# Moving a few element-wise operations of a fused kernel's set-up from VectorE to GpSimd

## The chip, the cores and the metric

The kernel runs on one core of one Trainium2 chip. A core has five engines that each work through their own list of instructions in order and wait for one another by semaphores: TensorE (PE in the profile, with its weight loads as PEld), VectorE (DVE), ScalarE (ACT), GpSimd (POOL) and SyncE (SP, which here only issues transfers). The metric is the device time of one execution in microseconds, as a median of runs.

## The reference, cut to what matters

The program is one gated cross-attention block followed by a mixture of experts, for 8 sequences (x: 8 x 512 x 256, context: 8 x 1024 x 192). The part that the change touches prepares a convolution filter (an S4D kernel) from parameters alone, once for all sequences:

```python
dt = jnp.exp(log_dt)
A = A_re + 1j * A_im                                # 256 x 64
dtA = dt[:, None] * A
dC = C * (jnp.exp(dtA) - 1.0) / A
powers = jnp.exp(dtA[:, :, None] * jnp.arange(L))   # L = 512
K = 2.0 * jnp.einsum('dn,dnl->dl', dC, powers).real
y = irfft(rfft(x) * rfft(K))[:, :L] + x * D_skip
```

Beside it, and independent of it, stands attention in which each row of scores (1024 wide, 4 heads) keeps its 32 largest entries, takes a softmax over them and is averaged over the heads. Later stages need both: attention's result modulates the normalised x, the filter is applied in the frequency domain, and then come a feed-forward layer, one shared expert and one of 8 routed experts per token.

## The kernel before, in words

**The loop over sequences.** At line 1394 the kernel runs several streams side by side for each sequence b: the attention of b (`attention`, line 905), the layers behind the attention of b - 1 (`behind`), and the preparation of b + 1 (`prepare`, line 431). For b = 0 there is nothing behind it, and its place is taken by `setup` (line 604), which computes the filter and loads the small weights. So the set-up lies beside the attention of the first sequence, and must be over before `mixed` (line 1057) of sequence 0 can use the filter (`kf`, line 556).

**The set-up.** Its first part works on 128 x 256 tiles, all of them slices of one tile `us` (`small`, line 676) or of `ats` (the four transposed parameters) and `dds`. It ends in the coefficient dC, whose real and imaginary parts `dcr` and `dci` become `uu` and `vv`, two slices of `dds`. Then comes a loop of 8 steps over 32 channels each (line 731). The power exp(dtA l) is split into l = 32 a + c. Each step builds, for 16 values of a, the angles' tiles `ta`, `tk` and the growth `tp` (128 x 512), and for 32 values of c the tiles `qa`, `qk`, `qq` (128 x 1024). GpSimd makes the products with the indices, VectorE reduces the angle to one turn (a rounding into `tk` or `qk`, and a subtraction), ScalarE takes sines and exponentials, and then `tk` and `ta` are scaled by `uu` and `vv`, added (line 750) and multiplied into `tp`; on the other side `qq` is multiplied by `qk` (line 762). TensorE multiplies `qq` with `tp` into `pz`, 32 small products a step, and ScalarE copies the result into `ktime`. After the last step come two rounds of matrix products with the Fourier table, which give `kf`.

**Attention.** A step works on 128 rows and two of the four heads, so a sequence takes 8 steps. TensorE makes the scores `pS`, ScalarE copies them to `sc`, VectorE pairs them by maximum and minimum into `mn`, reduces into `hi`, and GpSimd prunes with two integer operations on `mn` (lines 944 and 945). VectorE then finds the largest eight of a row four times (MAX8 and MATCH_REPLACE8), ScalarE takes exponentials into `e`, VectorE masks and sums them (`e<-sc,t,e`), ScalarE scales them, and GpSimd adds the heads into `acc` (line 983). At the end of 128 rows TensorE transposes `acc` (`pa`) and multiplies it with the context `cx` into `pu`.

**The order of the work.** Nothing is issued while the kernel's functions run. Each operation is noted with an estimated cost (`time`, line 137), and `order` (line 220) then lists them as a planner does: it goes through time, and gives each engine, among the operations that could begin, the one with the smallest number in the order of the streams. The costs enter only there. Each engine then works through its own list strictly in order. So changing an operation's engine changes the two lists directly and, by the planner's times, the order of others. Tiles come from pools with few buffers: `ta`, `tk`, `tp` have two each, `qa` and `qk` one each, and `qq` takes its turn with the weights of later layers in a pool of five.

**Line numbers.** Almost all operations go through one helper, so the profile gives them all line 323. They are told apart by their tiles.

Of the kernel before, what the change touches and what calls it, by code (L numbers as in the profile page):

```python
# [334 lines left out]
def bc(ap, axis, n):  # L335

    ap = ap.unsqueeze(axis)
    shape = list(ap.shape)
    shape[axis] = n
    return ap.broadcast_to(shape)  # L340
# [3 lines left out]
def tile_kernel(ctx: ExitStack, tc: tile.TileContext, a: dict, out: bass.AP):  # L344
# [45 lines left out]
    V, S, GP, TE, SY = (plan.engine(n, e) for n, e in (  # L390
        ("DVE", nc.vector), ("ACT", nc.scalar), ("POOL", nc.gpsimd), ("PE", nc.tensor), ("SP", nc.sync)))
# [4 lines left out]
    def bank(name, pool=ps_mm, tag="mm"):  # L396
        return pool.tile([P, 512], F32, tag=tag, name=name)
# [206 lines left out]
    def setup():  # L604
# [58 lines left out]
        ar, ai, cr, ci = (at[n] for n in ("A_re", "A_im", "C_re", "C_im"))  # L663
# [12 lines left out]
        def small(tag):  # L676
            return us[:, int(tag[1]), :]
# [13 lines left out]
        er, ei = small("u2"), small("u0")  # L691
# [4 lines left out]
        xr, xi, w1 = small("u3"), small("u4"), small("u1")  # L696
        V.tensor_mul(xr, cr, er)
        V.tensor_mul(w1, ci, ei)
        V.tensor_sub(xr, xr, w1)
        V.tensor_mul(xi, cr, ei)  # L700
        V.tensor_mul(w1, ci, er)
        V.tensor_add(xi, xi, w1)
        a2, w2 = small("u5"), small("u2")
        V.tensor_mul(a2, ar, ar)
        V.tensor_mul(w2, ai, ai)
# [2 lines left out]
        dcr, dci = small("u0"), small("u1")  # L708
# [1 line left out]
        V.tensor_mul(w2, xi, ai)  # L710
        V.tensor_add(dcr, dcr, w2)
        V.tensor_mul(dcr, dcr, a2)
        V.tensor_mul(dci, xi, ar)
        V.tensor_mul(w2, xr, ai)
        V.tensor_sub(dci, dci, w2)
        V.tensor_mul(dci, dci, a2)


        lo, hi = slice(0, NST), slice(NST, 2 * NST)
# [11 lines left out]
        for s in range(D // DC):  # L731
            ds = slice(s * DC, (s + 1) * DC)

            def big(pool, tag, n, name):
                return pool.tile([P, DC * n], F32, tag=tag, name=f"{name}{s}").rearrange(
                    "p (d n) -> p d n", n=n)


            ta, tk, tp = big(pk, "ga", NA, "ta"), big(pk, "sg", NA, "tk"), big(pk, "t2", NA, "tp")
            GP.tensor_mul(ta, bc(tn[:, ds], 2, NA), bc(ioa, 1, DC))  # L740
            GP.tensor_mul(tp, bc(dr[:, ds], 2, NA), bc(ioa, 1, DC))
            V.tensor_scalar(tk, ta, MAGIC, MAGIC, ALU.add, ALU.subtract)
            V.tensor_sub(ta, ta, tk)
            S.activation(tk, ta, AF.Abs)
            S.activation(tk, tk, AF.Sin, bias=hpi, scale=-2.0 * PI_IN)
            S.activation(ta, ta, AF.Sin, scale=2.0 * PI_IN)
            S.activation(tp, tp, AF.Exp)
            GP.tensor_mul(tk, tk, bc(uu[:, ds], 2, NA))
            GP.tensor_mul(ta, ta, bc(vv[:, ds], 2, NA))
            V.tensor_add(tk, tk, ta)  # L750
            GP.tensor_mul(tp, tp, tk)

            qa, qk, qq = big(pr, "xe", NCC, "qa"), big(pr, "hT", NCC, "qk"), big(wpool, "w", NCC, "qq")
            GP.tensor_mul(qa, bc(tn[:, ds], 2, NCC), bc(ioc[:, :NCC], 1, DC))
            GP.tensor_mul(qq, bc(dr[:, ds], 2, NCC), bc(ioc[:, :NCC], 1, DC))
            V.tensor_scalar(qk, qa, MAGIC, MAGIC, ALU.add, ALU.subtract)
            V.tensor_sub(qa, qa, qk)
            S.activation(qk[lo], qa[lo], AF.Abs)
            S.activation(qk[lo], qk[lo], AF.Sin, bias=hpi[lo], scale=-2.0 * PI_IN)
            S.activation(qk[hi], qa[hi], AF.Sin, scale=2.0 * PI_IN)  # L760
            S.activation(qq, qq, AF.Exp)
            V.tensor_mul(qq, qq, qk)
            pz = bank(f"pz{s}")
            for d in range(DC):
                TE.matmul(pz[:NCC, d * NA : (d + 1) * NA], qq[:, d, :], tp[:, d, :],
                          start=True, stop=True)

            z = pz[:NCC].rearrange("p (d t j) -> p j t d", t=NF, j=NA // NF)
            for j in range(NA // NF):
                S.copy(ktime[j * NCC : (j + 1) * NCC, :, ds], z[:, j])  # L770
            yield
# [621 lines left out]
    for b in range(B):  # L1393
        streams = [(some(att, n_att), n_att), behind(b - 1) if b else (setup(), n_set)]
        if b + 1 < B:
            streams.append((states[b + 1].prep, n_prep))
        together(*streams)
# [84 lines left out]
```

## Time and profile before

The time before is 1792.7 us, the median of 3 runs (1792.55 to 1793.37). The profiled execution took 1794.11 us, of which the page's span (first to last instruction) is 1792.3 us.

| | busy us | share of the span |
|---|---|---|
| PE | 1513.1 | 84% |
| DVE | 1302.1 | 73% |
| ACT | 1154.6 | 64% |
| POOL | 931.5 | 52% |

The averages hide the stages. The set-up loop runs in the window from about 65 to 227 us; a table by window stands in the prediction. In the answers below, a line of a group or of a timeline reads: engine, operation, output tile, inputs, sizes, number of instructions, busy time and mean; in brackets or after the bar, the idle time of the engine just before it and what ended that. A tile's answer gives the shortest, median and longest of its instructions, and when the first and the last began.

### The profile page before, as it was taken

What the parts mean: (1) busy time and instruction counts of PE and PEld (TensorE: products, weight loads), DVE (VectorE), ACT (ScalarE), POOL (GpSimd) and SP (SyncE); (2) the same over time, 40 slices, a digit from 0 to 9 for tenths busy, and PEclk for the clock granted to TensorE, in tenths of its full rate; (3) what the DMA queues carried; (4) which work ended last, traced back from release to release, by engine and by line L of the source; (5) the groups of instructions that cost most, each with busy time, mean ns of one, the idle gap of its engine ahead of it and who ended that gap; (6) DMA issues with size and microseconds to landing.
All of it is one profiled execution on the core that took longest, in us unless ns stands there. A gap on an engine that the chain in (4) does not pass through costs nothing. (4 is left out here: it accounts for less than half of the span.)

```text
span 1792.3 us, 21191 instructions
## 1 busy us (share of the span) xinstructions
PE 1513.1 (84%) x6363; PEld 893.1 (50%) x6363; DVE 1302.1 (73%) x3073; ACT 1154.6 (64%) x2008; POOL 931.5 (52%) x1072
## 2 busy tenths in 40 slices
PE   5365577797998798999889999998999989889885
PEld 2143333344543454465436554654465547547685
DVE  6989977885878697977798889697978987222210
ACT  4778844676747774887578877885788678123121
POOL 5578544445363645465555765474557646233122
PEclk8555677786998799998989999998999989989898
DMA  4000110001200120143103330431033205523794
GB/s 118 0 1 24 33 35 18 12 12 47 70 20 12 47 65 18 36 128 96 54 12 109 91 102 12 135 107 58 12 111 107 66 12 162 179 103 86 228 280 117
DMA packets 101289, 131.68 MB, mean 73 GB/s; under 512 B 9687, under 2 KB 73004, under 8 KB 101166
## 3 DMA queue, kind: packets, MB, share of 16 engines
q1 hardware_dynamic: 93102, 121.05, 21.1%
q0 software_dynamic: 7008, 8.42, 2.6%
q8 instruction: 52, 0.85, 0.2%
q10 hardware_dynamic: 1056, 0.79, 0.1%
q14 instruction: 71, 0.58, 0.1%
HBM read 112.22 MB, written 18.78 MB: 73 GB/s over the span
## 5 line engine op out<-in xcount | busy, mean ns | idle before, releaser
L323 PE MATMUL pS<-kT,qT 32*128 32x512 f32 x512 | 285.6, 742 | 71.2 <-DVE mn L323 61.0
L323 POOL TENSOR_TENSOR acc<-acc,e 128x1024 f32<-128x1024 f32 x96 | 229.0, 2385 | 182.3 <-ACT e L323 179.9
L323 DVE MAX8 top<-mn 128x8 f32<-128x256 f32 (+1 forms) x512 | 276.0, 556 | 11.9
L323 ACT COPY sc<-pS 128x512 f32<-128x512 f32 x256 | 145.6, 584 | 167.1 <-PE pS L323 136.9
L323 DVE SCALAR_TENSOR_TENSOR e<-sc,t,e 128x1024 f32<-128x1024 f32 x128 | 180.3, 1421 | 40.6 <-ACT e L323 40.3
L323 DVE TENSOR_TENSOR mn<-sc,pS 128x512 f32<-128x512 f32 x256 | 165.2, 677 | 35.9 <-PE pS L323 19.9
L323 POOL TENSOR_TENSOR mn<-mn 128x256 int32<-128x256 int32 x128 | 102.4, 800 | 164.4 <-DVE hi L323 163.8
L323 PEld LDWEIGHTS pS<-kT,qT 32*128 32x128 f32 x512 | 75.9, 208 | 203.6 <-DVE mn L323 98.9
L323 ACT ACTIVATE e<-sc,sm 128x1024 f32<-128x1024 f32 x128 | 145.1, 1146 | 16.1 <-POOL acc L323 13.2
L323 ACT ACT_TABLE_LOAD x118 | 151.4, 1283 | 4.0 <-issue 2.0
L323 PE MATMUL pm<-hT,w 128*128 128x512 f32 x256 | 137.9, 677 | 13.6 <-ACT hT L323 13.6
L323 ACT ACTIVATE junk<-sc,sm 128x1024 bf16<-128x1024 f32 x128 | 146.1, 1141 | 1.3
L323 PEld LDWEIGHTS pu<-aT,cx 128*96 128x96 f32 x1024 | 122.2, 168 | 28.6 <-issue 24.1
L323 PE MATMUL pu<-aT,cx 128*96 128x128 f32 x1024 | 135.4, 282 | 0.2 <-ACT aT L323 0.2
L323 PE MATMUL am<-w,ga 128*128 128x256 f32 x512 | 129.1, 398 | 6.1 <-ACT ga L323 6.1
L323 PEld LDWEIGHTS am<-w,ga 128*128 128x128 f32 x512 | 96.9, 196 | 51.4 <-issue 27.6
L323 POOL DMA_INDIRECT out_dram<-yb,to x38 | 61.5, 1620 | 96.7 <-DMA out_dram<-yb,to 46.3
L323 ACT ACTIVATE e<-e,sm 128x1024 f32<-128x1024 f32 x96 | 108.5, 1147 | 1.6 <-DVE sm L323 1.6
L323 POOL TENSOR_TENSOR mn<-mn,hi 128x256 int32<-128x256 int32 x128 | 104.9, 819 | 8.0
L323 DVE TENSOR_TENSOR ger<-sgr,pu 128x512 f32<-128x512 f32 x38 | 26.0, 684 | 108.7 <-PE pu L323 105.9
L323 DVE MATCH_REPLACE8 mn<-top,mn 128x256 f32<-128x256 f32 x256 | 104.6, 409 | 0.0
L323 POOL TENSOR_TENSOR yf<-yf,t 128x512 f32<-128x512 f32 (+1 forms) x80 | 85.2, 1089 | 35.0 <-DVE t L323 33.7
(287 smaller groups left out, 3125.0 us busy)
## 6 DMA issues: line engine op xcount, KB each, us to landing
rt_gate<-in_L_ffn_rt_gate_dram SPq DMA_DIRECT2D x38, 512.0 KB
rt_up<-in_L_ffn_rt_up_dram SPq DMA_DIRECT2D x38, 512.0 KB
rt_down<-in_L_ffn_rt_down_dram SPq DMA_DIRECT2D x38, 512.0 KB
w<-in_L_xattn_W_dram SPq DMA_DIRECT2D x32, 512.0 KB
cx<-in_ctx_dram SPq DMA_DIRECT2D x7, 768.0 KB
xtab<-zt SPq DMA_DIRECT2D x8, 642.5 KB
xb<-xtab SPq DMA_DIRECT2D x38, 128.5 KB
xt<-in_x_dram SPq DMA_DIRECT2D x8, 512.0 KB
```

The source lines that it names most:

```text
L323: o.fn()
```

## The change

In the loop, the addition of the two angle terms into `tk` (128 x 512) and the product of `qq` with `qk` (128 x 1024) go from VectorE to GpSimd, in each of the 8 steps. In the first part, seven operations on 128 x 256 go the same way: three that make `xi`, and four that make `dci`. As two engines would now write the same scratch slice, a new slice `w3` (the eighth of `us`, unused so far) is taken for the moved ones. Results, tiles and transfers are otherwise the same.

```diff
-        V.tensor_mul(xi, cr, ei)
-        V.tensor_mul(w1, ci, er)
-        V.tensor_add(xi, xi, w1)
+        w3 = small("u7")
+        GP.tensor_mul(xi, cr, ei)
+        GP.tensor_mul(w3, ci, er)
+        GP.tensor_add(xi, xi, w3)
...
-        V.tensor_mul(dci, xi, ar)
-        V.tensor_mul(w2, xr, ai)
-        V.tensor_sub(dci, dci, w2)
-        V.tensor_mul(dci, dci, a2)
+        GP.tensor_mul(dci, xi, ar)
+        GP.tensor_mul(w3, xr, ai)
+        GP.tensor_sub(dci, dci, w3)
+        GP.tensor_mul(dci, dci, a2)
...
             GP.tensor_mul(ta, ta, bc(vv[:, ds], 2, NA))
-            V.tensor_add(tk, tk, ta)
+            GP.tensor_add(tk, tk, ta)
             GP.tensor_mul(tp, tp, tk)
...
             S.activation(qq, qq, AF.Exp)
-            V.tensor_mul(qq, qq, qk)
+            GP.tensor_mul(qq, qq, qk)
```

## The prediction

> **What bounds the kernel now.** I read the page first (DVE and PE high, shares that are averages over stages), then a table of windows, since the change touches only the set-up. The four windows run from the second attention step of sequence 0 (its first `mn` at 69.8 us) to the first `mn` of sequence 1 (273.5 us):
>
> ```profile
> 69.80:121.30 51.50, 27.67 (x186) 17.67 (x187) 44.05 (x74) 35.14 (x57) 34.46 (x27) 0.52 0.00 1
> 121.30:172.20 50.90, 25.17 (x219) 15.96 (x218) 47.52 (x79) 44.12 (x70) 39.66 (x25) 0.55 0.07 21
> 172.20:223.00 50.80, 31.79 (x196) 18.96 (x195) 46.70 (x72) 44.19 (x69) 31.13 (x22) 0.58 0.10 29
> 223.00:273.50 50.50, 36.33 (x154) 16.83 (x152) 40.55 (x103) 23.75 (x43) 21.79 (x23) 0.76 0.10 32
> sum 203.70, PE 120.96 PEld 69.42 DVE 178.82 ACT 147.19 POOL 127.04; mean PE 30.24 PEld 17.36 DVE 44.71 ACT 36.80 POOL 31.76
> ```
>
> Columns after the length: busy us of PE, PEld, DVE, ACT and POOL, TensorE's granted clock, the share of DMA, GB/s. VectorE is busy 178.8 of 203.7 us (88%), GpSimd 127.0 (62%), ScalarE 147.2 (72%). TensorE mostly waits, and no transfer matters (DMA share 0.10 or less). So VectorE is the fullest engine of this stage, but ScalarE is not far behind. Later TensorE is:
>
> ```profile
> 700.00:900.00 200.00, 187.25 (x734) 105.92 (x733) 164.81 (x410) 151.01 (x264) 116.02 (x138) 0.95 0.24 70
> 1300.00:1500.00 200.00, 190.24 (x807) 115.31 (x806) 169.33 (x419) 155.76 (x258) 114.51 (x133) 0.97 0.25 76
> ```
>
> From there on nothing changes: set side by side, the planned lists of all engines are alike from the first attention step of sequence 1 to the end, and differ only before it. The later weights' loads start when a tile comes free, so they move with the work. I therefore carry a shift of the 273.5 us point to the end one to one. The chain of waits shown on the page reaches back only to 1646 us, so it says nothing against or for this.
>
> **What is removed from VectorE.** The groups of 50 to 275 us:
>
> ```profile
> L323 DVE SCALAR_TENSOR_TENSOR e<-sc,t,e 128x1024 f32<-128x1024 f32 x16 | 24.9, 1579 | 0.0
> L323 DVE TENSOR_TENSOR qq<-qq,qk 128x1024 f32<-128x1024 f32 x8 | 13.8, 1726 | 5.4 <-ACT qk L323 5.4
> L323 DVE TENSOR_TENSOR qa<-qa,qk 128x1024 f32<-128x1024 f32 x8 | 13.4, 1672 | 0.2
> L323 DVE TENSOR_TENSOR ta<-ta,tk 128x512 f32<-128x512 f32 x8 | 12.9, 1616 | 0.2
> L323 DVE TENSOR_SCALAR qk<-qa 128x1024 f32<-128x1024 f32 x8 | 9.0, 1129 | 0.4 <-POOL qa L323 0.4
> L323 DVE TENSOR_TENSOR tk<-tk,ta 128x512 f32<-128x512 f32 x8 | 9.0, 1126 | 6.2 <-POOL ta L323 6.0
> L323 DVE TENSOR_SCALAR tk<-ta 128x512 f32<-128x512 f32 x8 | 7.5, 935 | 0.0
> ```
>
> The product `qq<-qq,qk` takes 13.8 us and the sum `tk<-tk,ta` 9.0: 22.8 us of work. VectorE also idles 5.4 and 6.2 us just before these two, because it reaches them before their inputs are there: 11.6 us of idle time that leave its list with them. The seven small operations on 128 x 256 take, by the timeline, 1.18 us (0.75 for two, 0.43 for one) for `xi` and 1.63 for `dci`: 2.8 us. GpSimd's `xi` needs about 2.2 us, while VectorE does `xr` and the 1/|A|^2 part (over 3 us), so VectorE hardly waits for it; `dci`, some 2.9 us on GpSimd, runs beside `dcr`, but then `uu` and `vv` need it. I take 2 of the 2.8 us (bounds -1, if the wait for `dci` outlasts the saving, and 2.8).
>
> **What is added to GpSimd.** No row has these two there. The nearest are GpSimd's two-input products of the same sizes, and VectorE's own as a yardstick (shortest, median, longest ns):
>
> ```profile
> L323 POOL TENSOR_TENSOR tk<-tk,dds x8: 1053/1058/2035, 82.1 to 211.3; 128x512 f32<-128x512 f32 x8
> L323 POOL TENSOR_TENSOR qa<-us,ioc x8: 1907/2500/2951, 66.6 to 208.4; 128x1024 f32<-128x1024 f32 x8
> L323 DVE TENSOR_TENSOR qq<-qq,qk x8: 1224/1322/2928, 86.6 to 220.5; 128x1024 f32<-128x1024 f32 x8
> ```
>
> Undisturbed, a step adds 1.06 + 1.91 = 2.97 us, 8 steps 23.8; by the means of these groups in the stage (1.20 and 2.45) 29.2. The Trainium skill speaks against the move: "GPSIMD Engine Reference", section 4.1, Engine selection, gives element-wise work to VectorE, GpSimd being about 2 times slower with two inputs. The shortest times here say 1907/1224 = 1.56. By the rule the undisturbed addition would be an estimated 2 x 8 x (1.22 + 0.67) = 30 us; by the rows 24, with the collisions of this stage 29. I take 27. The seven small ones add 7 x 0.73 = 5.1 us before the stage (a 96 x 256 product takes 0.73). GpSimd becomes 127.0 + 27 = 154 us: 79% of a stage of 194. It issues no transfer in this stage, so none is held up. On the SP queue nothing is added; four small loads (`b`, `vt`) come to stand ahead of four large weight loads, which takes away GpSimd's 17 us wait for `b`, worth nothing, as what follows it was ready only then.
>
> **What the remaining work of VectorE loses.** The two engines get in each other's way:
>
> ```profile
> 159.69 2.72 DVE L323 SCALAR_TENSOR_TENSOR e<-sc,t,e 128x1024 f32<-128x1024 f32 x1
> ```
>
> ```profile
> 158.38 2.95 POOL L323 TENSOR_TENSOR qa<-us,ioc 128x1024 f32<-128x1024 f32 x1 [1.64 <-ACT qk L323]
> ```
>
> Alone they take 1.27 and 1.91 us. MAX8, MATCH_REPLACE8 and operations that read scores from `pS` keep their times beside GpSimd; those with two inputs in SBUF, and the roundings, do not. Their excess over the shortest of their kind: e 24.9 - 16 x 1.27 = 4.6; qa 13.4 - 8 x 1.22 = 3.6; ta 12.9 - 8 x 0.69 = 7.4; qk 9.0 - 8 x 0.68 = 3.6; tk 7.5 - 8 x 0.41 = 4.2: 23.4 us. GpSimd's busy share goes from 62% to 79%, times 1.27: 6 us more. The skill's "SBUF — State Buffer", section "SBUF: two separate sides", calls this an exclusive lock held for a whole instruction. If every added us on GpSimd kept VectorE out, that would be 27, which would eat the move; but VectorE's operations of this kind have only 42 us of undisturbed work in the stage (14 x 1.27 + 8 x 3.0), about a fifth of the time, and a fifth of 27 is 5.4. Both ways about 6; bounds 3 and 15.
>
> **New waits.** This is the term with the widest bounds. Attention's pruning (`mn` on GpSimd, 14 pairs in the stage) stands in the same in-order list, now behind up to one product and one sum more; behind it wait MATCH_REPLACE8 on VectorE, then the exponentials' masks, ScalarE's scaling and the next `pS`. Such a wait exists already:
>
> ```profile
> 235.45 0.09 DVE L323 MATCH_VALUE_LOAD mn<-top,hi 128x8 f32 x1 [3.14 <-POOL mn L323]
> ```
>
> If each of 14 prunings meets half of a step's added 2.97 us, that is 21 us. The other way, too: `qq` is now in GpSimd's list behind waits for sines (`qk` from ScalarE), and holds what is behind it. And the planned list puts the last step of the loop later against attention: the last `pz` now stands behind scores of sequence 1, and VectorE's `kf` work behind the third block's masks, so VectorE can idle for the chain product, `pz` (3.6 us), copy (1.0), first Fourier product (1.9). Against that, ScalarE has four table loads fewer in its list (15 for 19, 4 x 1.28 = 5 us). From 0 (the planner interleaves the waits with other work) to 35 us; I take 20, near the 21.
>
> **Sum.** 22.8 + 11.6 + 2 removed, 6 and 20 added: 10.4 us less. The profiled execution's span would be 1792.3 - 10.4 = 1781.9 us, its time 1794.1 - 10.4 = 1783.7; the median lies 1.4 under that execution, so 1782.3, which I call 1782.5.
>
> **The rivals.**
> - *GpSimd becomes the fullest engine and holds attention up* (slower). Of its 76.7 us idle, 17 are the wait for `b`; the waits for ScalarE, TensorE and VectorE in its list make up the rest, about 59. If they stay, the stage takes 154 + 59 = 213 us instead of 203.7: 9 us slower, some 1802. It decides when new waits pass 30 us, 2.1 us a pruning. For it: the list is in order, and the sum and the product wait for ScalarE. Against: 79% is less than the 88% at which VectorE ran.
> - *The waits eat the gain* (30 us, within 3.6): about 1792.5. The engines' shares would then be even at about 80%, which is hard to pack in order.
> - *The waits are well hidden*, 5 us: 25 us less, about 1767. ScalarE's 142 us in a stage of 179 (79%) would allow it.
> - *The shift does not reach the end*: TensorE is the limit later and had work left over. Against: TensorE's lists need attention of sequence 0 and the filter first, and it idled in the stage. I give it no number of its own; it falls under "the same".
>
> **How the numbers follow.** Likeliest, about 10 us less: 0.50; well hidden: 0.11; the same: 0.14; slower: 0.25. The likeliest alone spans 1777 to 1789, faster than the 3.6 us (0.2%) that a measurement can tell from none. So faster 0.61, same 0.14, slower 0.25. For 8 in 10, the range goes from 1768 (most of the well-hidden case) to 1802 (the slower case's own number); what is left out is half of each.
>
> **What would show it.** Right: the first `mn` of sequence 1 near 263 us; VectorE busy about 162 us in the stage up to there, GpSimd about 154; the sum at 1.1 to 1.3 us and the product at 1.9 to 2.5 on GpSimd; VectorE's waits for GpSimd's `mn` some 20 us; later windows alike. Wrong: waits for `mn` over 30 us; a product well over 2.5 us; VectorE's excess over 30 us; or an early shift that shrinks between 300 and 1500 us.

## The result, and the profile after

The changed kernel takes 1798.35 us in the median, the kernel before, on the same chip, 1793.03: a ratio of 1.0035 with a 95% interval of 1.002 to 1.005. That is 5 to 6 us slower where 10 us faster was forecast. One of its 14 runs, at 2982.85 us, counts as slow and is left out of the ratio. The profiled execution of the changed kernel took 1795.14 us with a span of 1793.4 (before: 1794.11 and 1792.3). Two comparisons of the same two kernels differ by a quarter of a per cent (a second one, below, gave 1.0011), so what I say of the change is that it gains nothing and costs some 2 to 6 us; the interval of the second comparison also holds no change at all.

The stage in which the prediction was made, from the second attention step of sequence 0 to the first `mn` of sequence 1, now runs from 70.56 to 275.61 us. I call the end of it the join. The table by windows of the kernel after, four quarters of the stage (columns as before):

```profile
70.56:121.80 51.24, 30.11 (x181) 18.45 (x182) 41.94 (x78) 35.81 (x56) 39.36 (x29) 0.50 0.00 1
121.80:173.10 51.30, 25.80 (x163) 13.55 (x163) 45.58 (x75) 39.38 (x63) 42.31 (x28) 0.57 0.06 21
173.10:224.30 51.20, 29.70 (x192) 18.11 (x190) 41.80 (x73) 39.45 (x68) 42.17 (x31) 0.60 0.06 19
224.30:275.61 51.31, 36.45 (x219) 19.43 (x219) 38.53 (x85) 26.84 (x46) 31.83 (x26) 0.80 0.13 42
sum 205.05, PE 122.06 PEld 69.54 DVE 167.85 ACT 141.47 POOL 155.66; mean PE 30.52 PEld 17.38 DVE 41.96 ACT 35.37 POOL 38.92
```

VectorE went from 178.82 us of work to 167.85, GpSimd from 127.04 to 155.66: the work did move. But the stage is 1.4 us longer, and VectorE now idles 205.05 - 167.85 = 37.2 us in it, where it idled 24.9. No engine is full any more: 82%, 76% and 69% for VectorE, GpSimd and ScalarE. The later windows are as they were:

```profile
700.00:900.00 200.00, 187.05 (x734) 105.69 (x733) 164.64 (x409) 149.56 (x262) 114.17 (x137) 0.95 0.24 70
1300.00:1500.00 200.00, 190.31 (x791) 113.88 (x790) 169.33 (x416) 154.29 (x257) 114.41 (x130) 0.97 0.25 75
```

The groups of 50 to 275 us of the kernel after, those that answer to the ones shown of before:

```profile
L323 DVE SCALAR_TENSOR_TENSOR e<-sc,t,e 128x1024 f32<-128x1024 f32 x16 | 27.0, 1694 | 9.4 <-ACT e L323 9.3
L323 POOL TENSOR_TENSOR qq<-qq,qk 128x1024 f32<-128x1024 f32 x8 | 20.0, 2498 | 1.3 <-ACT qk L323 1.2
L323 DVE TENSOR_TENSOR qa<-qa,qk 128x1024 f32<-128x1024 f32 x8 | 16.5, 2061 | 0.3
L323 DVE TENSOR_TENSOR ta<-ta,tk 128x512 f32<-128x512 f32 x8 | 15.4, 1926 | 0.2
L323 POOL TENSOR_TENSOR tk<-tk,ta 128x512 f32<-128x512 f32 x8 | 10.8, 1349 | 0.6
L323 DVE TENSOR_SCALAR tk<-ta 128x512 f32<-128x512 f32 x8 | 9.1, 1142 | 0.3 <-POOL ta L323 0.3
L323 DVE TENSOR_SCALAR qk<-qa 128x1024 f32<-128x1024 f32 x8 | 8.5, 1057 | 2.4 <-POOL qa L323 2.4
```

Three things are to be seen. The two moved operations cost GpSimd 20.0 + 10.8 = 30.8 us. The operations that stayed on VectorE grew: `qa` from 13.4 to 16.5, `ta` from 12.9 to 15.4, the rounding `tk` from 7.5 to 9.1, `e` from 24.9 to 27.0. And the mask `e`, which before did not wait (0.0 in its row), now waits 9.3 us for ScalarE. In the view of waits (VectorE, 65 to 280 us) the first rows of the kernel before were

```profile
DVE tk L323 <- POOL ta L323: 6.0, 4, 3.1
DVE qq L323 <- ACT qk L323: 5.4, 5, 2.3
DVE mn L323 <- POOL mn L323: 3.5, 2, 3.1
```

and those of the kernel after put the wait for ScalarE first, ahead of GpSimd's `mn`, which I had expected to lead:

```profile
DVE e L323 <- ACT e L323: 9.3, 5, 3.5
DVE mn L323 <- POOL mn L323: 7.8, 1, 7.8
DVE wf L323 <- PE p_wf L323: 5.7, 3, 3.5
DVE kf L323 <- PE pf L323: 4.4, 1, 4.4
```

(Columns: us in total, times, the longest.) The one wait for `mn` is of the kind foreseen. This is GpSimd's timeline in front of it, with the sum and the product in the way:

```profile
106.42 1.26 POOL L323 TENSOR_TENSOR tk<-tk,ta 128x512 f32<-128x512 f32 x1
107.76 1.27 POOL L323 TENSOR_TENSOR tp<-tp,tk 128x512 f32<-128x512 f32 x1
109.46 2.35 POOL L323 TENSOR_TENSOR qq<-qq,qk 128x1024 f32<-128x1024 f32 x1 [0.42 <-ACT qk L323]
111.77 0.72 POOL L323 TENSOR_TENSOR mn<-mn 128x256 int32<-128x256 int32 x1
```

VectorE stood for the prune until 112.52 (idle 7.76 us). The waits for ScalarE are of another kind. VectorE's timeline:

```profile
204.91 0.74 DVE L323 MAX8 top<-hi 128x8 f32<-128x256 f32 x2
209.12 1.56 DVE L323 SCALAR_TENSOR_TENSOR e<-sc,t,e 128x1024 f32<-128x1024 f32 x1 [3.47 <-ACT e L323]
```

and ScalarE's at the same time:

```profile
197.06 1.28 ACT L323 ACT_TABLE_LOAD   x1
198.35 0.72 ACT L323 ACTIVATE tk<-tk,hpi 128x512 f32<-128x512 f32 x1
...
202.35 0.61 ACT L323 ACTIVATE ta<-ta 128x512 f32<-128x512 f32 x1
...
206.65 1.28 ACT L323 ACT_TABLE_LOAD   x1
207.94 1.15 ACT L323 ACTIVATE e<-sc,sm 128x1024 f32<-128x1024 f32 x1
```

ScalarE takes six sines and cosines of the set-up, of two steps, in one run from 198.35 to 202.96 us. The lines left out after it are a copy and attention's own work, its counts (`junk`) above all, up to the second table load; only then comes the exponential that attention waits for. VectorE's list has nothing between 205.65 and the mask. The next wait, 3.07 us in front of the mask at 213.76, has no sine before it: there the exponential stands behind the copies of `pz` into `ktime`, which wait for TensorE. So what the two waits have in common is the place of the exponential in ScalarE's list, behind work of the set-up. The four table loads that the new lists save (12 for 16 in the trace from 65 to 276 us, which the prediction wrote down as a gain) do mean fewer and longer stretches of sines, but length alone is not shown to be the cause: before, too, ScalarE took a run of 4.4 us (153.87 to 158.30), and VectorE did not wait for the exponential after it.

### The profile page after: what moved, and what is told of

It is laid out like the page before. It is cut to its first block, busy times and chain, and to the rows that moved or that the text cites. A ratio compares the mean times of both kernels' runs of the same rounds, so it can differ in the third digit from the quotient of the medians.

```text
span 1793.4 us, 21187 instructions
## 1 busy us (share of the span) xinstructions
PE 1515.7 (85%) x6363; PEld 894.6 (50%) x6363; DVE 1291.6 (72%) x3050; ACT 1148.4 (64%) x2004; POOL 964.7 (54%) x1095
## 5 line engine op out<-in xcount | busy, mean ns | idle before, releaser
L323 PE MATMUL pS<-kT,qT 32*128 32x512 f32 x512 | 289.6, 736 | 90.0 <-DVE mn L323 77.7
L323 DVE MAX8 top<-mn 128x8 f32<-128x256 f32 (+1 forms) x512 | 276.1, 556 | 13.5 <-POOL mn L323 1.5
L323 PE MATMUL pm<-hT,w 128*128 128x512 f32 x256 | 138.1, 678 | 13.4 <-ACT hT L323 13.4
L323 PE MATMUL pu<-aT,cx 128*96 128x128 f32 x1024 | 139.3, 286 | 5.4 <-ACT aT L323 5.4
L323 PEld LDWEIGHTS pu<-aT,cx 128*96 128x96 f32 x1024 | 124.9, 171 | 33.8 <-issue 24.1
```

Of the source, the lines that this page charges most:

```text
L323: o.fn()
```

## The experiments

Theory A, the prediction's own: VectorE's list bounds the stage, and what decides is how much GpSimd's added work takes back, by its time and by collisions. Theory B: the order that the planner makes of the changed engines holds the stage up by itself, whatever GpSimd needs. Since an operation can be planned as if on one engine and executed on another, or executed in a narrow form, or not at all, the order and the work can be changed apart. An operation that is executed elsewhere stands in the other engine's list where the plan has it in time. "Old order" and "new order" mean the planned lists of the kernel before and of the kernel after. Ratios are to the kernel before on the same chip, with 95% intervals; its medians beside the runs below are 1794.58 to 1794.87 us, and the quotient of two medians differs from the ratio by up to 0.16%. The join is that of one profiled execution, which is 273.5 us before; an unchanged kernel's join can differ by 4 us from one execution to the next (275.6 and 279.6 for the kernel after), and what comes after the join took from about 1515 to 1526 us in these runs, so a verdict rests on the ratio first.

### The kernel after, again

> The changed kernel again, for a second profiled execution beside the parts: 3 to 7 us slower than before, the first score pairing of sequence 1 at 275 to 279 us. If the loss arises after that point instead, the pairing stays at 275 us and the rest is longer than the 1518 us of the profiled executions so far.

Measured: 1797.06 us, ratio 1.0011 [0.9996, 1.0025], join 279.6 us. Its stage:

```profile
71.07:279.57 208.50, 125.61 (x751) 70.62 (x751) 168.38 (x309) 141.48 (x231) 156.04 (x111) 0.59 0.06 20
```

The first comparison's interval began at 1.002. By the two ratios the change is 0.1 to 0.35% slower, and neither interval comes near a gain of 0.6%.

### One part of the change at a time

```diff
-            V.tensor_add(tk, tk, ta)
+            GP.tensor_add(tk, tk, ta)
```

> Only the sum goes to GpSimd (8 x 1.3 us there, 9 us off VectorE with 6 us of idle time ahead of it). GpSimd theory: a third of the added time, so between 5 us faster and 2 us slower. Order theory: no forecast from the engines' times; any sign, but with a pairing of sequence 1 that doesn't follow the added time.

```diff
-            V.tensor_mul(qq, qq, qk)
+            GP.tensor_mul(qq, qq, qk)
```

> Only the product goes to GpSimd (8 x 2.5 us there). GpSimd theory: two thirds of the added time, 1 to 6 us slower than before, and worse than the sum alone. Order theory: any sign.

The third has the changed kernel's seven small operations on GpSimd, and sum and product on VectorE:

> Only the seven small operations go to GpSimd. The profile of the changed kernel has the second attention step 0.8 us later (70.6 for 69.8 us), as VectorE's own small products there collide with GpSimd's. So 0 to 2 us slower than before if that is passed on; 0 if the loop has room for it; 2 us faster by the prediction's term.

Measured: the sum alone 1798.21 us, 1.0028 [1.0015, 1.0041], join 276.1; the product alone 1791.33, 0.9978 [0.9964, 0.9993], join 271.0; the small ones alone 1793.03, 0.9983 [0.9973, 0.9994], join 272.4. The part that puts least on GpSimd in the loop (10.8 us) is the slow one, and the one that puts most there (20.0 us) is a little faster. GpSimd's load does not rank them, and both loop parts went against what theory A had set for them. Each of the three has lists of its own from the planner, so this pointed to the order, and did not prove it.

### The moved work in the old order

```diff
+    VG = plan.engine("DVE", nc.gpsimd)
...
-            V.tensor_add(tk, tk, ta)
+            VG.tensor_add(tk, tk, ta)
...
-            V.tensor_mul(qq, qq, qk)
+            VG.tensor_mul(qq, qq, qk)
```

Sum and product are planned as VectorE's and executed by GpSimd; the small operations stay on VectorE.

> The sum and the product run on GpSimd, but every engine's list keeps the order of the kernel before (the seven small operations stay on VectorE). If the new order of the lists is what took the gain back, this gains about 10 us, with the first score pairing of sequence 1 near 263 us. If it is the time put on GpSimd (its collisions with VectorE and the waits behind it), this does no better than the changed kernel: 0 to 10 us slower than before, the pairing at 274 us or later.

Measured: 1803.59 us, 1.0066 [1.0048, 1.0084], join 286.5. Its stage, and VectorE's waits in it:

```profile
70.50:286.50 216.00, 122.52 (x751) 69.45 (x751) 157.85 (x310) 146.72 (x235) 148.64 (x111) 0.59 0.07 20
```

```profile
DVE mn L323 <- POOL mn L323: 21.6, 6, 7.9
DVE qk L323 <- POOL qa L323: 16.2, 3, 6.2
DVE qk L323 <- POOL qq L323: 5.0, 1, 5.0
```

VectorE has 21 us less work than before and idles 58.2 us instead of 24.9. Here the engine waits for GpSimd almost alone, 42.8 us in these three rows. Without a new plan the move costs 12 us. That is theory A's outcome, and a little beyond its range: in the old order it is GpSimd's added work that holds the stage up, and theory B's gain of 10 us did not come. So the planner's answer to the move is a real one: it takes off 6 to 10 of them.

### The new order with the old engines

```diff
+    GV = plan.engine("POOL", nc.vector)
...
-            GP.tensor_add(tk, tk, ta)
+            GV.tensor_add(tk, tk, ta)
...
-            GP.tensor_mul(qq, qq, qk)
+            GV.tensor_mul(qq, qq, qk)
```

The seven small operations likewise: all nine kinds are planned as GpSimd's and executed by VectorE.

> Every operation is on VectorE as before, but the lists have the order planned for the change. Order theory: the order alone costs, so this is at least 10 us slower than before, about 12 us on top of the gain that is then missing. GpSimd theory: the order is only unsuited to VectorE's fuller list; VectorE gets its 23 us back but loses 12 us of collisions and most of the 24 us of new waits, so between 10 us faster and 5 us slower.

Measured: 1798.88 us, 1.0029 [1.0015, 1.0043], join 278.7; VectorE idle 37.8 us. The order alone costs some 5 us, as much as the whole change, with every operation where it was. That is half of what theory B had set (at least 10) and at the edge of what theory A allowed (5), so this run alone does not decide between them.

### The two operations narrowed to one column

```diff
+    def thin(eng, real, method, *v):
+        plan.note(eng, method, partial(getattr(real, method), *(x[:, :, 0:1] for x in v)), v, {})
...
-            GP.tensor_add(tk, tk, ta)
+            thin("POOL", nc.gpsimd, "tensor_add", tk, tk, ta)
...
-            GP.tensor_mul(qq, qq, qk)
+            thin("POOL", nc.gpsimd, "tensor_mul", qq, qq, qk)
```

That is the new order, on GpSimd. Only the first column of each is computed, so the filter is another one. The same edit of the kernel before, with "DVE" and `nc.vector`, is the old order, on VectorE.

> The changed kernel's lists, with the moved sum and product cut to one of 16 or 32 columns (the rest of the sum and of the product is left out), so GpSimd's time for them nearly vanishes. GpSimd theory: collisions and waits go with it, 15 to 25 us faster than before, VectorE's idle time in the stage down from 37 us to about 20. Order theory: still within 5 us of the changed kernel, as the lists are the same.

> The lists of the kernel before, with the sum and the product on VectorE cut to one of 16 or 32 columns (the rest is left out). It tells what taking 22.8 us of work from VectorE is worth when nothing is put in its place. If VectorE bounds the stage, 15 to 23 us faster. If the stage is bound by chains through ScalarE and TensorE, which VectorE only fills up, under 10 us.

Measured: new order 1792.2 us, 0.9988 [0.9976, 1.0001], join 272.1; old order 1785.48, 0.9954 [0.9938, 0.9969], join 266.3. In the old order the two narrow kinds still took 3.8 + 5.2 = 9.0 us (some of them stretch beside GpSimd; see the last section), so 13.8 us of VectorE's work were gone, and 7.2 arrived at the join. The waits in front of these two operations did not go with their work: 7.5 us in front of `qq` and 8.1 in front of `tk`, where there had been 5.4 and 6.0. In the new order almost nothing is gained although GpSimd has hardly more to do than before (128.6 us): theory A had 15 to 25 us, with VectorE's idle time down to about 20 us, and it is 43.8.

### The two operations left out

```diff
+    def none(eng, method, *v):
+        plan.note(eng, method, lambda: None, v, {})
...
-            V.tensor_add(tk, tk, ta)
+            none("DVE", "tensor_add", tk, tk, ta)
...
-            V.tensor_mul(qq, qq, qk)
+            none("DVE", "tensor_mul", qq, qq, qk)
```

That is the old order; in the new one it is "POOL", from the kernel after.

> The kernel before, its lists in the same order, but the sum and the product of each step are not issued at all (so the filter is another one): 22.8 us of VectorE's work are gone, and so are the 5.4 and 6.2 us that VectorE stood in front of them. If VectorE's list bounds the stage, as the prediction had it, the join (first mn of sequence 1) comes up to 22.8 + 11.6 = 34 us earlier, about 1760. If, as the narrow versions let me think (13.8 us less work gave 7.2 at the join), a good part of what is taken away comes back as waits for ScalarE, TensorE and GpSimd, it is 12 to 16 us: some 1779 to 1783.

> The kernel after, its lists in the same order, but the sum and the product are not issued on any engine (another filter). It is the floor of the new order: with the narrow ones on GpSimd it stood 2 us under the kernel before. If the new order itself holds the stage up, the floor is only 3 to 6 us under the kernel before, about 1789 to 1792, and well above the same edit in the old order. If the order costs nothing, both edits give the same time.

Measured: old order 1783.89 us, 0.9929 [0.9905, 0.9954], join 262.2; new order 1795.05, 0.9993 [0.9978, 1.0008], join 273.4. What follows the join took 1520 and 1521 us (1518.8 before), so the other filter costs nothing there. Leaving the two out also drops the waits of what follows on them, so each of these times is, if anything, too good for the work alone. The old order came out at the lower of its two forecasts (12 to 16 us), the new one still below its own (3 to 6 us): it gains about 1. The stages, old order first:

```profile
70.50:262.20 191.70, 118.63 (x751) 67.24 (x751) 158.67 (x310) 146.17 (x235) 123.23 (x95) 0.62 0.07 22
```

```profile
70.70:273.40 202.70, 120.17 (x751) 69.20 (x751) 159.77 (x311) 141.44 (x231) 121.60 (x95) 0.62 0.07 21
```

The two have the same work on VectorE within a microsecond, and nothing of the moved work on GpSimd. Eleven microseconds lie between them, and only the order of the lists and the place of the seven small operations differ; these moved alone cost nothing. VectorE's waits in the old order (65 to 280 us; up to its join at 262.2 the row of `mn` is 8.1 us):

```profile
DVE qk L323 <- POOL qa L323: 11.0, 3, 6.2
DVE mn L323 <- POOL mn L323: 10.9, 6, 3.1
DVE wf L323 <- PE p_wf L323: 4.4, 3, 2.1
```

and in the new one:

```profile
DVE e L323 <- ACT e L323: 17.4, 7, 4.0
DVE wf L323 <- PE p_wf L323: 6.0, 3, 4.0
DVE kf L323 <- PE pf L323: 4.3, 1, 4.3
```

The row at the top of the kernel after, `e` waiting for ScalarE, is still there with the moved work gone altogether, and larger: 17.4 us. It comes from the order, not from GpSimd's added work. The longest of these waits, 4.03 us before the second mask at 121.22, has this on ScalarE:

```profile
114.71 1.15 ACT L323 ACTIVATE e<-sc,sm 128x1024 f32<-128x1024 f32 x1
118.44 1.05 ACT L323 COPY ktime<-pz 32x128 f32<-32x128 f32 x4 [2.58 <-PE pz L323]
119.52 0.63 ACT L323 ACTIVATE tp<-tp 128x512 f32<-128x512 f32 x1
120.06 1.13 ACT L323 ACTIVATE e<-sc,sm 128x1024 f32<-128x1024 f32 x1
```

The second exponential stands behind the set-up's copy, and the copy waits for TensorE. For the kernel as planned, this run decides for theory B: in the new order, sum and product could cost nothing on any engine and the kernel would stand where it stood before. In the old order it is GpSimd's work that costs, as theory A has it, though leaving that work out gives only a third of what VectorE's list promised.

### All in one table

Ratio to the kernel before, and the join in us. The seven small operations are on VectorE in the old order and on GpSimd in the new one, except in the new order's third row, where they are on VectorE:

| sum and product | old order | new order |
|---|---|---|
| left out | 0.9929, 262.2 | 0.9993, 273.4 |
| one column | 0.9954, 266.3 (VectorE) | 0.9988, 272.1 (GpSimd) |
| on VectorE | 1, 273.5 | 1.0029, 278.7 |
| on GpSimd | 1.0066, 286.5 | 1.0035 and 1.0011, 275.6 and 279.6 |

### A version that keeps the sum on VectorE

The product and the small operations were each a little faster alone, so both were moved, and the sum was left (the kernel after with `V.tensor_add(tk, tk, ta)`). Beside it ran a version with the same lists in which VectorE executes the product.

> The product and the small operations on GpSimd, the sum stays on VectorE. Alone they gave 0.9978 and 0.9983. If gains add, 0.996 of the kernel before, some 7 us less. If what decides is the order that the planner makes of the changed costs, they need not add: anywhere from 0.996 to 1.003.

> The lists of the version with product and small operations moved, but the product is executed by VectorE at its place (the small ones stay on GpSimd). If that version's gain comes from work taken off VectorE, this one gives it back and stands at the kernel before or above it. If it comes from the order alone, this one is as fast or faster.

Measured: 1791.32 us, 0.9982 [0.997, 0.9995], join 268.7; with the product on VectorE 1793.63, 0.9991 [0.9974, 1.0008], join 273.2. The gains do not add. With that order, moving the product gives 4.5 us at the join of one execution, but the two ratios' intervals overlap, so whether the order or the move makes the 0.2% was not settled. At about 0.2%, the least that this measurement can tell from none, these and the product alone (0.9978) are the best versions found.

## Why the prediction was wrong

**The sum, term by term.** In the trace of the kernel after, the terms came out as follows (us at the join).

| term of the prediction | forecast | measured |
|---|---|---|
| work taken off VectorE | -22.8 | -22.8 |
| idle time removed, and new waits | -11.6 + 20 = +8.4 | 37.2 - 24.9 = +12.3 |
| what VectorE's other work loses | +6 | 167.85 - (178.8 - 22.8) = +11.9 |
| small operations | -2 | 70.56 - 69.80 = +0.8 |
| sum | -10.4 | +2.2 (the join moved from 273.5 to 275.6) |

Three terms missed by 4, 6 and 3 us, all to the same side, and each within the bounds given to it. But busy and idle time always add up to the stage, so this splits the number and does not give the cause.

**The step that failed: "What is removed from VectorE".** It took 22.8 us of work and 11.6 us of idle time and let both reach the end one to one, because VectorE was the fullest engine (88%). With both really gone and nothing put in their place, in the same order, the stage gave 12.0 us and the kernel 0.71%, that is 12.7 us, of the 34.4. VectorE's busy time fell by 20.1 us, but the stage only by 12.0, because VectorE's idle time grew from 24.9 to 33.0: the waits in front of the two operations turned into waits for `qa` and `mn` further on. So VectorE, 88% busy and waiting by turns for three others, was not the only bound of this stage, and most of the idle time in front of the two operations did not go with them: it belonged to inputs that came late. In the new order the same removal gave 1.0 us. Set against the runs without the two operations, the forecast comes apart like this (us of the stage, without the small operations; the second figure is the second trace of the kernel after; single executions, with about 4 us between two of the same kernel):

| term | forecast | old order | new order |
|---|---|---|---|
| the two operations removed, nothing put in their place | -34.4 | -12.0 | -1.0 |
| then on GpSimd: VectorE's other work | +6 | -0.8 | +8.1, +8.6 |
| then on GpSimd: VectorE's idle time | +20 | +25.1 | -5.7, -2.8 |
| sum | -8.4 | +12.3 | +1.4, +4.8 |

In the old order the price of the move was about right (24.3 for 26) and only the gain was wrong. In the kernel as planned the price was much smaller than feared, 2.4 to 5.8 us, and the gain was gone before the price came.

**"New waits" had about the right size by luck, and the wrong cause.** 20 us were set against the removed 11.6, on the argument that the prunings stand behind products and sums in GpSimd's list. In the old order that is exactly what happens: waits for `mn` 21.6 us, against 21 by the working, and beside them 16.2 and 5.0 for `qa` and `qq`, for which I had no term. In the new order, which is the kernel, waits for `mn` are 7.8 us, and the idle time is as long with the sum and the product left out: 202.7 - 159.8 = 42.9 us. The prediction read the new lists, and named the last step of the loop standing later and four table loads fewer; it costed the first within the 0 to 35 us and the second as a help of 5 us. That exponentials would stand in ScalarE's list behind the set-up's sines and copies, and VectorE behind them, it did not see.

**What the other work loses.** 11.9 us instead of 6. By the rows, `qa` grew by 3.1, `ta` by 2.5, `tk` by 1.7, `e` by 1.6 in the stage, and two kinds of `kf` by 1.9. Of the 11.9 us, 3.8 are there in the new order with sum and product left out (159.8 against 156.0), so GpSimd's added work accounts for 8.1, near the forecast; the argument was that GpSimd's share of time rises by a fifth. But which operations meet is a matter of the lists: in the old order, with 31.8 us of sums and products more on GpSimd, VectorE's remaining work was 157.9 us, no more than without them (158.7). There VectorE waits instead. The mark that the prediction set for being wrong here was passed: by its own measure (each kind's sum less its shortest, in the groups of 50 to 275 us, where there are 16 masks for the 14 of the stage) the excess is 6.7 for `e`, 6.7 for `qa`, 9.9 for `ta`, 3.1 for `qk` and 5.8 for `tk`, 32.2 us against 30.

**GpSimd's own time.** 27 us were taken, 30.8 measured. The row chosen for the product (`qa<-us,ioc`, 1907 ns) was the wrong one: both its operands are repeated along an axis. The trace of before had a product of two full tiles, `tp<-tp,tk`, at 1261 ns, and the sum has just that. The shortest of the two moved kinds:

```profile
L323 POOL TENSOR_TENSOR tk<-tk,ta x8: 1261/1268/1602, 83.9 to 230.6; 128x512 f32<-128x512 f32 x8
```

```profile
L323 POOL TENSOR_TENSOR qq<-qq,qk x8: 2350/2357/3322, 88.5 to 239.1; 128x1024 f32<-128x1024 f32 x8
```

Against VectorE's 0.67 and 1.22 us this is 1.9 times, so the rule of about 2 that the prediction weighed (the Trainium skill, "GPSIMD Engine Reference", section 4.1, Engine selection) agrees with these runs, and the 1.56 of the rows that I chose does not. It weighs little: 3.8 us on an engine that still had 49 us idle in the stage.

**The small operations.** The stage begins 0.8 us later instead of 2 earlier. Of this, 0.25 us lie before them (the first `mn` starts at 36.47 and 36.72 us). From there to the start of the stage it takes 33.3 us in each of the six traces that have them on VectorE in the order of the kernel before or in that of one loop part, and 33.8 in each of the seven that have them on GpSimd, so they cost 0.5 (or 1.75 against the new order with them on VectorE, 32.1). What stayed on VectorE ran beside them, and two such operations rose from 0.75 us to 1.80 by the timeline of the kernel after:

```profile
54.91 1.80 DVE L323 TENSOR_TENSOR us<-ats,us 128x256 f32<-128x256 f32 x2
```

Alone, without sum and product, they gave 0.9983, so this term is small either way.

**What held.** Of the signs that the prediction set, GpSimd's busy time (154 set, 155.7 measured), the times of the sum and the product there (1.26 and 2.36 us in the middle) and the later windows came as said, and the first `mn` of sequence 1 (263 set, 275.6 measured), VectorE's busy time (162, 167.9) and its waits for `mn` (20, 7.8) did not. The shift of the join arrives at the end about one to one: joins of 262.2, 286.5 and 278.7 us (-11.3, +13.0 and +5.2) stand beside ratios worth -12.7, +11.8 and +5.2 us. The wait for `b` on GpSimd went, as forecast; what it was worth was not tried apart. Of the rivals, "GpSimd holds attention up" came nearest in time (some 1802 forecast); its mechanism is that of the old order, 1.0066, and not the main one of the kernel as planned. The rival that was missing is the order itself. Which of the planner's choices makes the new order worse when the work is gone was not taken apart further; the runs show where VectorE waits, not which single exchange of two operations is to blame.

## What to carry to other kernels

Where a planner orders the lists, a move between engines is two edits: where the work runs, and what order comes of it. Run them apart, by planning for one engine and executing on the other, before a cause is named; here the order alone cost what the whole change cost. And before crediting an engine with the time taken off it, run the version in which the operations are simply left out: here that ceiling was a third of the sum in the old order (12.7 of 34.4 us) and about nothing in the new one, where no price on the other engine, however low, could have made the move pay.

## What the runs showed of the hardware

A GpSimd sum or product of two full f32 tiles took 1261 ns for 128 x 512 and 2350 ns for 128 x 1024. Products with one or both operands repeated along an axis took less: 1047 and 1907 ns. That the repetition is the reason is the likely reading; it was not tried apart.

Narrowing an operation to 32 elements a row does not always make it short beside GpSimd. In the narrow version in the old order, VectorE's sums took 197 to 1904 ns:

```profile
L323 DVE TENSOR_TENSOR tk<-tk,ta x8: 197/466/1904, 85.2 to 208.7; 128x32 f32<-128x32 f32 x8
```

The longest began while GpSimd had just started a product, and ended with it:

```profile
114.69 1.90 DVE L323 TENSOR_TENSOR tk<-tk,ta 128x32 f32<-128x32 f32 x1 [1.49 <-POOL ta L323]
114.62 1.91 POOL L323 TENSOR_TENSOR qa<-us,ioc 128x1024 f32<-128x1024 f32 x1
```

This holds for all 16 narrow sums and products of that trace: the seven that took 0.41 us or more began during a GpSimd instruction and ended 0.06 to 0.08 us after it, whatever its length, and the nine of 0.20 to 0.22 us began while GpSimd was idle. So an instruction of VectorE with both inputs in SBUF can hold a wait for GpSimd that the profile counts as its busy time, which fits the exclusive lock that the prediction weighed.
